# A gathered table as two float32r halves instead of three bfloat16 parts, in a graph network on one Trainium2 core

## The chip, the cores and the metric

The kernel runs on one core of one Trainium2 chip. The core has five engines that run their own instruction streams: TensorE (PE) multiplies, VectorE (DVE) and ScalarE (ACT) work elementwise, GpSimd (POOL) here issues the indirect transfers (gathers and scatters), and SyncE (SP) issues the plain ones. Sixteen DMA engines carry out all transfers. Tables between the stages lie in device memory (HBM); on the core there is the on-chip memory of 128 partitions and the accumulators (PSUM) that PE writes. The metric is the device time of one execution in microseconds; less is better.

## The reference, cut to what matters

Inputs are 6250 nodes of 256 features and a graph of 50,000 random pairs taken in both directions and 6250 self loops, 106,250 edges in all, sorted by their target node. There are four steps, each added to x:

```python
x = x + gnn0(layernorm(x), edges, ...)      # two sums over neighbours (256 and 512 wide), with dense layers
x = x + attention(layernorm(x), ...)        # slice tokens: 8 heads of 64 tokens over all nodes
x = x + gnn1(layernorm(x), edges, ...)      # one sum over neighbours, 256 wide
x = x + ffn1(layernorm(x), ...)             # the 2 best of 8 experts for each node

def gnn1(x, src, dst):
    src, dst = concatenate([src, loop]), concatenate([dst, loop])   # self loops once more
    h = x @ W
    deg = segment_sum(ones, dst); dinv = rsqrt(deg)
    out = segment_sum(h[src] * (dinv[src] * dinv[dst])[:, None], dst) + b
    return relu((out - running_mean) * rsqrt(running_var + eps) * gamma + beta)
```

The change concerns gnn1's sum over neighbours. The kernel first sums the rows of layernorm(x) times dinv[src] and multiplies by W afterwards, which gives the same.

## The kernel before, in words

Nodes are worked on in 49 tiles of 128, edges in chunks of 128. A sum over neighbours is made by PE: for one chunk, GpSimd gathers the 128 source rows into an on-chip tile (one edge per partition), VectorE makes a 128 x 128 matrix of zeros and ones that has a one where an edge goes to a node, and PE multiplies the two and accumulates over the chunks of a tile. So that bfloat16 products give a float32 result, a row of a table is stored as three bfloat16 parts that add up to the float32 number (`split`, L370), and each chunk takes three products (`multiply`, L179, its matmul in L183).

The class `Sums` (L187) does this for all three sums. It keeps a ring of on-chip tiles for gathered rows (`depth` of them, `message` L207). In `__call__` (L233) for a tile, gathers are issued ahead until chunk c + depth (L162 by way of L244); for every half-step k (some 8 chunks of targets from half a tile) `hot` (L219) makes the zeros and ones for its chunks with one VectorE instruction (L227); then come the products, and after the half-step `add` puts the sum where it belongs. Other work is let in between chunks through `between`.

The stages of the program are: layer norm and a plan of the edges (to 150 us); the first sum with its dense layers (to about 1330); the second sum, of which every third half-step gathers float32 rows and multiplies them as float32 (L253), with the logits and tokens of the attention (to about 2520); the core of the attention (to 2549); deslicing (to 2650); and the third stage (to the end).

Deslicing (the loop that ends in the write to T3, L1315 to L1335) goes over groups of four tiles: eight float32 products per pair of tiles (L1325), the addition to x1 (L1327), the layer norm times dinv, the `split` into three parts (two copies on ScalarE, L372 and L375, and two differences on VectorE, L373 and L376), and the write of the group to table T3 through ScalarE's queue (L1335). Each group's slice weights are loaded at its head.

The third stage runs in a block in which the order of SP, PE, ACT and DVE is the order written (`manual_schedule`); GpSimd's order is laid down by `in_order`. A ring of 14 tiles (`sums = Sums(others, T3, msgs, 14, ...)`, L1362) holds rows of T3. The self loops are not in the 782 chunks of this sum: each tile of sums `s3s[t]` is loaded ahead from S3, a table of zeros unless edges lie beyond the plan (`load_ahead`, 7 buffers), VectorE adds the tile's own rows to it (L1701), and `add3` (L1353 to L1359) the accumulated products. Two tiles at a time then pass through `choice`: transposes of s3 (L387), the product with W (`pn`, L1393), the layer norm, transposes, the product with the gate (`pg`, L1414), VectorE's choice of the two best experts, the places of the rows (`pp`, L1453), and four indirect writes of the rows into the experts' regions (`send`, L1472). As soon as an expert has 128 rows, a block is due: SP fetches its rows and biases (four blocks ahead), PE transposes (`pt`, L1579), multiplies by the first weights (`ph`, L1585), ScalarE copies and applies relu (L1587 to L1594), PE multiplies by the second (`py`, L1599), VectorE adds the bias (L1600) and SP stores the rows. There are 112 such blocks; their pieces are let in between the chunks, seven slots per tile. The eight experts' weights, 16 loads, come in at the stage's head. At the end GpSimd gathers for each tile the two rows of its experts' outputs (`g`, L1637, 8 buffers), and VectorE adds them with their shares (L1638).

Of the kernel before, what the change touches and what calls it, by code (L numbers as in the profile page):

```python
# [9 lines left out]
F32 = mybir.dt.float32  # L10
BF16 = mybir.dt.bfloat16
I32 = mybir.dt.int32
AF = mybir.ActivationFunctionType
OP = mybir.AluOpType
AX = mybir.AxisListType
# [2 lines left out]
P = 128  # L18
# [3 lines left out]
def gin_transolver_gcn_moe(ctx: ExitStack, tc: tile.TileContext, a: dict, out: bass.AP):  # L22
# [13 lines left out]
    nc = tc.nc  # L36
    x, src, dst = a["x"], a["src"], a["dst"]
    N, D = x.shape
# [32 lines left out]
    class Chunks:  # L71

        def __init__(self, edges):
            self.n, self.per = -(-edges // P), -(-edges // N)
            assert all(self.start(k) < self.start(k + 1) for k in range(2 * NT - 1))

        def start(self, k):

# [8 lines left out]
    T1 = dram.tile([NP, 3 * D], BF16, name="T1")  # L87
    T1f = dram.tile([NP, D], F32, name="T1f")
    T2 = dram.tile([NP, 3 * HID], BF16, name="T2")
    T3 = dram.tile([NP, 3 * D], BF16, name="T3")  # L90
    T2f = dram.tile([NP, HID], F32, name="T2f")
    kept = dram.tile([P, NCP], I32, name="kept_src"), dram.tile([P, NCP], F32, name="kept_dst")
    flat = [dram.tile([P, NCH2], F32, name="flat" + n) for n in ("src", "dst")]
# [93 lines left out]
    class Sums:  # L187
# [4 lines left out]
        def __init__(self, edges, table, pool, depth, hots, ps, add, ones=0, whole=None, is_whole=lambda k: k % 3 == 1):  # L192
            self.whole, self.whole_at = whole, is_whole
            self.edges, self.start = edges, edges.start
            self.table, self.hots, self.ps, self.add, self.ones = table, hots, ps, add, ones
            W = table.shape[1]
            self.F = W // 3
            self.ring = [pool.tile([P, W + 4 * ones], BF16, name=f"msg{i}") for i in range(depth)]
            self.of = [None] * depth
            self.hotf = None  # L200
            self.n, self.made, self.beside = 0, {}, None
            self.early, self.each = False, None
# [16 lines left out]
        def hot(self, k, c0):  # L219

            if (k, c0) not in self.made:
                n = min(HOTS, self.start(k + 1) - c0)
                if self.is_whole(k):
                    hot = self.hotf[k % 2] if self.hotf else self.hots.tile([P, HOTS, P], F32, name="hotf", bufs=2)
                else:
                    hot = self.hots.tile([P, HOTS, P], BF16, name="hot")
                nc.vector.scalar_tensor_tensor(  # L227
                    hot[:, :n, :], self.edges.dst[:, c0:c0 + n, None].to_broadcast([P, n, P]), float(k * HALF),
                    node2[:, k % 2, None, :].to_broadcast([P, n, P]), op0=OP.subtract, op1=OP.is_equal)
                self.made[k, c0] = hot  # L230
            return self.made[k, c0]

        def __call__(self, t, between=None, times=7):  # L233

            ks = range(2 * t, min(2 * t + 2, 2 * NT - 1))
            lo, hi = self.start(ks[0]), self.start(ks[-1] + 1)
            done = 0
            for k in ks:
                pa = self.ps.tile([P, 512], F32, name="pa", tag="agg", bufs=2)
                for c in range(self.start(k), self.start(k + 1)):  # L240
                    while self.n < min(c + len(self.ring), self.edges.n):
                        of = next(u for u in range(k, 2 * NT) if self.n < self.start(u + 1))
                        table = self.whole if self.is_whole(of) else self.table
                        ins = gather(self.message(self.n, of)[:, :table.shape[1]], table, self.edges.src[:, self.n:self.n + 1])  # L244
                        self.n += 1
                        if self.beside is not None:
                            in_order(ins)
                            self.beside(t)
                    c0 = c - (c - self.start(k)) % HOTS
                    hot, msg, ends = self.hot(k, c0)[:, c - c0, :], self.message(c, k), (c == self.start(k), c == self.start(k + 1) - 1)  # L250
                    if self.is_whole(k):
                        n = self.F + self.ones
                        self.last = nc.tensor.matmul(pa[:, :n], hot, msg[:, :n], start=ends[0], stop=ends[1])  # L253
                    else:
                        self.last = multiply(pa, hot, msg, self.F, *ends, self.ones)
                    if self.each is not None:
                        self.each(c)
                    if self.early and c == self.start(k) + 2 and k + 1 < 2 * NT - 1:
                        self.hot(k + 1, self.start(k + 1))
                    while between is not None and done < (c + 1 - lo) * times // (hi - lo):  # L260
                        between()
                        done += 1
                self.added = self.add(k, pa)
# [17 lines left out]
    def rest(table, add, n_of, count=None, begin=None, kept=None):  # L281


        n = nc.values_load(n_of[0:1, 0:1], min_val=0, max_val=NT)
        W = table.shape[1]
        with tc.tile_pool(name="rest", bufs=1) as w, tc.tile_pool(name="rest_ps", bufs=1, space=PSUM) as ps:
            with tc.For_i(0, n, 1) as t:
                t = nc.s_assert_within(t, 0, NT - 1)
                if begin is not None:
                    begin(t, w)  # L290
                src_of, dst_of = srcT, dstT
                if kept is not None:
                    src_of = w.tile([P, NCP], I32, name="srcT")
                    nc.sync.dma_start(src_of, kept[0])
                    dst_of = w.tile([P, NCP], F32, name="dstT")
                    nc.sync.dma_start(dst_of, kept[1])
                c0 = nc.values_load(bounds[0:1, ds(t, 1)], min_val=0, max_val=NCP)
                c1 = nc.values_load(bounds[0:1, ds(t + NT, 1)], min_val=0, max_val=NCP)
                with tc.For_i(c0, c1, 1) as c:
                    c = nc.s_assert_within(c, 0, NCP - 1)  # L300
                    ii = w.tile([P, 1], I32, name="ii")
                    nc.vector.tensor_copy(ii, src_of[:, ds(c, 1)])
                    parts_ = BF16 if table is not T1f else F32
                    msg = w.tile([P, W], parts_, name="msg")
                    gather(msg, table, ii)

                    k = w.tile([P, 8], F32, name="k")
                    nc.vector.tensor_tensor(k[:, 4:5], dst_of[:, ds(c, 1)], first[:, ds(t, 1)], op=OP.subtract)
                    hot = w.tile([P, P], parts_, name="hot")
                    nc.vector.tensor_scalar(hot, node, k[:, 4:5], None, op0=OP.is_equal)  # L310
                    pa = ps.tile([P, 512], F32, name="pa")
                    if parts_ is F32:
                        nc.tensor.matmul(pa[:, :W], hot, msg, start=True, stop=True)
                    else:
                        multiply(pa, hot, msg, W // 3, True, True)
                    add(t, pa, w)
                    if count is not None:
                        pc = ps.tile([P, 2], F32, name="pc")
                        nc.tensor.matmul(pc, hot, ones[:, :2], start=True, stop=True)
                        nc.vector.tensor_add(count[:, ds(t, 1)], count[:, ds(t, 1)], pc[:, 0:1])  # L320
# [26 lines left out]
    def layer_norm(work, xt, J, outs, times=None, sd=None, here=0):  # L347
# [14 lines left out]
        for j in range(J):  # L362
# [3 lines left out]
            else:  # L366
                nc.scalar.activation(outs[j], xt[:, j, :], AF.Identity, scale=sd[:, 0, j:j + 1],
                                     bias=sd[:, 1, j:j + 1])

    def split(parts, v, left, less):  # L370

# [659 lines left out]
    with tc.tile_pool(name="attn", bufs=1) as ap_:  # L1031
# [281 lines left out]
        with back, tc.tile_pool(name="desl_ps", bufs=2, space=PSUM) as ps:  # L1313
            w = bw
            for ts in groups(4, 5):  # L1315
# [4 lines left out]
                for j0 in range(0, J, 2):  # L1320
                    js = range(j0, min(j0 + 2, J))
                    p = ps.tile([P, 2, D], F32, name="po", tag="mm", bufs=4)
                    for j in js:
                        for m in range(KG):
# [4 lines left out]
                hs = w.tile([P, 4, D], F32, name="hs")  # L1329
                layer_norm(w, x1, J, [hs[:, j, :] for j in range(J)], dinv[:, ts[0]:ts[-1] + 1],  # L1330
                           ln3[:, :, ts[0]:ts[-1] + 1])
                hr = w.tile([P, 4, 3, D], BF16, name="hr")
                for _ in split(hr[:, :J], hs[:, :J, :], hs[:, :J, :], nc.vector.tensor_tensor):
                    pass
                nc.scalar.dma_start(block(T3, ts), hr[:, :J].rearrange("p j s f -> p j (s f)"))  # L1335
    right.close()
    effs.close()
# [21 lines left out]
            nc.vector.tensor_add(s3s[t][rows], s3s[t][rows], pa[rows, :D])  # L1359

    start = others.start
    sums = Sums(others, T3, msgs, 14, hots, ps, add3)  # L1362
    sent = [[] for _ in parts]
    taken = [[] for _ in parts]
    stored = [[] for _ in parts]
# [5 lines left out]
    def load_ahead(t):  # L1371

        for u in range(t, min(t + 5, NT)):
            if u not in s3s:
                s3s[u] = w.tile([P, D], F32, name="s3", bufs=7)
                nc.sync.dma_start(s3s[u], S3[u])

    def flush(keep):
# [246 lines left out]
    def combine(when):  # L1625
# [3 lines left out]
        o = xr[:r, t, :]  # L1629
        gs = []  # L1630
        for c in range(2):
            g = w.tile([P, D], F32, name="g", bufs=8)
            in_order(gather(g[:r], XD[i], place[:r, t, c:c + 1]))
            gs.append(g[:r])

# [119 lines left out]
```

## Time and profile before

| | us |
|---|---|
| median of three runs | 4216.75 (4215.5 to 4220.2) |
| profiled execution | 4227.88 |
| its span in the profile | 4225.7 |
| deslicing | 2549 to 2650 |
| third stage | 2650 to 4226 |

Mean granted clock of PE in the profiled execution: 0.838 of full speed.

How to read the lines: L183 is line 183 of the kernel. A group of instructions shows the engine, the operation, what it writes and reads by the program's names, the tile's shape and type, how often it occurs, then its busy time in us, the mean of one in ns, and the idle time of the engine ahead of it with what ended that time. PEld is PE's loading of weights (here the ones and zeros), which can lie beside a product. "Issue" is time in which the engine waited for nothing that the profile shows; "remote" is an event whose sender the profile doesn't show. In the page's rows of 40 slices each digit is the busy tenths of one slice (106 us), and PEclk the clock that was granted to PE, in tenths of full speed. A line of the waits gives the total us, the number of waits and the longest. A line of the timeline gives the start, the length, the engine and the number of instructions run together, and in brackets what ended the idle time before.

### The profile page before, as it was taken

How to read it: one execution, taken by the hardware profiler on the slowest of the kernel's cores; microseconds unless marked ns; L12 is line 12 of the kernel's file. 1: busy time of each engine (PE TensorE's matmuls, PEld its weight loads, DVE VectorE, ACT ScalarE, POOL GpSimd, SP SyncE). 2: the span in 40 equal slices, each digit the busy share in tenths (PEclk: the TensorE clock that was granted, in tenths of full speed). 3: DMA queues.
4: the chain of work that ended last, by engine and by line, in shares of the span. 5: the costliest groups of instructions: out<-in, count | busy, mean ns of one | idle time of the engine just before them, and what ended most of it. 6: DMA issues, size and time to landing. Idle time of an engine off the chain costs nothing. (4 is left out here: it accounts for less than half of the span.)

```text
span 4225.7 us, 42390 instructions
## 1 busy us (share of the span) xinstructions
PE 3043.9 (72%) x12790; PEld 1826.7 (43%) x12854; DVE 1553.9 (37%) x3988; ACT 863.7 (20%) x1737; POOL 2510.3 (59%) x2618
## 2 busy tenths in 40 slices
PE   3667777777786788788878779345677767667775
PEld 2334433333343444444444447234445545445543
DVE  5353222122222444344444447233333333333343
ACT  4111111111121111111111125011222222222332
POOL 4776666666664666666666630665656665666544
PEclk6788888888898889899988989667888888888977
DMA  7567767777676778777877755645545555555545
GB/s 257 164 209 230 223 219 231 221 222 220 219 241 245 262 265 262 247 252 260 272 254 248 245 170 178 223 136 149 157 147 152 153 158 153 155 158 163 158 123 154
DMA packets 356496, 861.49 MB, mean 204 GB/s; under 512 B 60104, under 2 KB 158674, under 8 KB 356266
## 3 DMA queue, kind: packets, MB, share of 16 engines
q0 software_dynamic: 174688, 611.60, 47.3%
q1 hardware_dynamic: 175066, 237.50, 16.4%
q10 hardware_dynamic: 6512, 9.63, 0.6%
q8 instruction: 106, 1.74, 0.2%
q14 instruction: 124, 1.02, 0.1%
HBM read 691.29 MB, written 167.21 MB: 203 GB/s over the span
## 5 line engine op out<-in xcount | busy, mean ns | idle before, releaser
L162 POOL DMA_INDIRECT msg<-T,srcT x2059 | 1976.5, 960 | 1363.3 <-issue 549.1
L183 PE MATMUL pa<-msg,hot 128*128 128x257 bf16 (+2 forms) x6114 | 1135.6, 323 | 194.0 <-issue 101.0
L183 PEld LDWEIGHTS <-hot 128*128 128x128 bf16 x6177 | 650.8, 106 | 795.1 <-issue 536.4
L162 POOL DMA_INDIRECT msg<-T2f,srcT x256 | 242.9, 949 | 138.8 <-PE pa L183 60.1
L1599 PE MATMUL py<-wx,hT 128*128 x896 | 257.0, 438 | 94.3 <-issue 90.5
L227 DVE SCALAR_TENSOR_TENSOR hot<-dstT,node 128x1024 bf16<-128x1024 f32 (+2 forms) x255 | 310.4, 1219 | 30.7 <-PE pa L183 20.1
L928 PE MATMUL p<-W2a,h2T 128*128 128x512 f32 x392 | 233.2, 679 | 66.6 <-issue 38.7
L1599 PEld LDWEIGHTS py<-wx,hT 128*128 128x128 f32 x896 | 197.9, 224 | 182.7 <-issue 149.6
L1585 PE MATMUL ph<-wx,xdT 128*128 x448 | 253.6, 695 | 28.9 <-ACT xdT L1581 13.3
L642 DVE TENSOR_TENSOR dinv<-dinv,pa 128x1 f32<-128x1 f32 x145 | 22.2, 153 | 658.9 <-PE pa L183 361.5
L253 PE MATMUL pa<-msg,hotf 128*128 128x512 f32 x512 | 255.9, 625 | 0.6 <-issue 0.3
L919 PE MATMUL p<-h1T,W1b 128*128 128x512 f32 (+2 forms) x480 | 221.1, 559 | 40.6 <-issue 21.4
L1600 DVE TENSOR_TENSOR yd<-py,wb 128x256 f32<-128x256 f32 x112 | 47.5, 425 | 435.7 <-PE py L1599 259.3
L1193 PE MATMUL ptok<-xn,sw 128*128 128x257 f32 (+1 forms) x392 | 123.8, 463 | 94.4 <-DVE sw L1182 47.2
L271 DVE SCALAR_TENSOR_TENSOR s<-s,own,pa 128x512 f32<-128x512 f32 x97 | 72.0, 742 | 224.2 <-PE pa L253 87.6
L1594 ACT ACTIVATE hT<-pt,wb 128x128 f32<-128x128 f32 x448 | 127.6, 369 | 126.0 <-remote 113.7
L909 PE MATMUL p<-h0T,W1a 128*128 128x512 f32 (+2 forms) x240 | 119.7, 598 | 43.9 <-issue 29.8
L1587 ACT ACTIVATE h<-ph 128x512 f32<-128x512 f32 x112 | 66.9, 598 | 405.7 <-remote 151.0
L1591 PE MATMUL pt<-ident,h 128*128 128x128 f32 x448 | 76.5, 297 | 101.0 <-ACT h L1587 57.7
L1193 PEld LDWEIGHTS ptok<-xn,sw 128*128 128x128 f32 (+1 forms) x392 | 87.7, 233 | 133.9 <-DVE sw L1182 55.8
L1168 PE MATMUL pl<-Weff,xnT 128*128 128x512 f32 x196 | 107.9, 691 | 47.3 <-issue 27.6
L162 POOL DMA_INDIRECT g<-XD,place x98 | 97.1, 991 | 70.5 <-DVE xr L1638 26.8
(379 smaller groups left out, 3644.4 us busy)
## 6 DMA issues: line engine op xcount, KB each, us to landing
XD<-zeros SPq DMA_DIRECT2D x204, 256.0 KB
msg<-T,srcT POOLq DMA_INDIRECT x2059
T<-tp SPq DMA_DIRECT2D x49, 384.0 KB
wb<-WB SPq DMA_DIRECT2D x112, 130.0 KB
xd<-XD SPq DMA_DIRECT2D x112, 128.0 KB
XD<-yd SPq DMA_DIRECT2D x112, 128.0 KB
T2f<-tf SPq DMA_DIRECT2D x49, 256.0 KB
s<-T2f SPq DMA_DIRECT2D x23, 512.0 KB
```

The source lines that it names most:

```text
L162: return nc.gpsimd.indirect_dma_start(out=msg, out_offset=None, in_=table, in_offset=bass.IndirectOffsetOnAxis(ap=ix, axis=0))
L183: ins = nc.tensor.matmul(pa[:, :n], hot, msg[:, s * F:s * F + n], start=(start and s == 2), stop=(stop and s == 1))
L227: nc.vector.scalar_tensor_tensor(hot[:, :n, :], self.edges.dst[:, c0:c0 + n, None].to_broadcast([P, n, P]), float(k * HALF), node2[:, k % ...
L253: self.last = nc.tensor.matmul(pa[:, :n], hot, msg[:, :n], start=ends[0], stop=ends[1])
L909: nc.tensor.matmul(p[:, :T], W1a[:, k, m * P:(m + 1) * P], h0T[:, k, :T], start=(k == 0), stop=(k == KD - 1))
L919: nc.tensor.matmul(p[:, :T], W1b[:, k, m * P:(m + 1) * P], h1T[:, k, :T], start=(k == 0), stop=(k == KH - 1))
L928: nc.tensor.matmul(p, h2T[:, k, j * P:(j + 1) * P], W2a[:, k, :], start=(k == 0), stop=(k == KH - 1))
L1168: nc.tensor.matmul(p, xnT[:, k, j * P:(j + 1) * P], Weff[:, k, :], start=(k == 0), stop=(k == KD - 1))
L1193: nc.tensor.matmul(p[:, :D + 1], sws[j][:r, m * P:(m + 1) * P], xn[:r, j, :], start=(j == 0), stop=(j == J - 1))
L1585: nc.tensor.matmul(p[:, :HID], xdT[:, k, :], W1[:, k, :], start=(k == 0), stop=(k == KD - 1))
L1594: nc.scalar.activation(hT[:, m, :], pt[:, m * P:(m + 1) * P], AF.Relu, bias=b1[:, m:m + 1])
L1599: nc.tensor.matmul(p[:, :D], hT[:, m, :], W2[:, m, :], start=(m == 0), stop=(m == KH - 1))
```

## The change

T3 holds float32 rows of 512 numbers, two halves of 256, instead of bfloat16 rows of 3 x 256: the first half is the number rounded to float32r, the second the difference from it, which float32r holds exactly. A row takes 2048 bytes instead of 1536. `halves_of` makes both with one copy and one difference per group of tiles. A chunk takes two products (`multiply_halves`) with ones and zeros in float32r. The ring has 10 tiles (of 2048 bytes) instead of 14 (of 1536). The tiles of ones and zeros hold `edges.most` chunks: 8 in the third sum, where they held 9 (`HOTS`), and 9 as before in the others. The tiles s3 and g share 8 buffers, where s3 had 7 and g 8. `rest` takes the new form too; it handles edges beyond the plan, of which these inputs have none.

```diff
+F32R = mybir.dt.float32r
...
+            self.most = -(-self.per // 2)
...
-    T3 = dram.tile([NP, 3 * D], BF16, name="T3")
+    T3 = dram.tile([NP, 2 * D], F32, name="T3")
...
-            self.F = W // 3
-            self.ring = [pool.tile([P, W + 4 * ones], BF16, name=f"msg{i}") for i in range(depth)]
+            self.halves = table.dtype == F32
+            self.F = W // 2 if self.halves else W // 3
+            self.ring = [pool.tile([P, W + 4 * ones], table.dtype, name=f"msg{i}") for i in range(depth)]
...
-                n = min(HOTS, self.start(k + 1) - c0)
+                n = min(self.edges.most, self.start(k + 1) - c0)
...
-                    hot = self.hots.tile([P, HOTS, P], BF16, name="hot")
+                    hot = self.hots.tile([P, self.edges.most, P], F32R if self.halves else BF16, name="hot")
...
+                    elif self.halves:
+                        self.last = multiply_halves(pa, hot, msg, self.F, *ends)
...
+    def multiply_halves(pa, hot, msg, F, start, stop):
+
+        for s in range(2):
+            ins = nc.tensor.matmul(pa[:, :F], hot, msg[:, s * F:(s + 1) * F].bitcast(F32R),
+                                   start=(start and s == 0), stop=(stop and s == 1))
+        return ins
+
+    def halves_of(parts, v):
+
+        nc.scalar.activation(parts[:, :, 0, :], v, AF.Copy)
+        nc.vector.tensor_tensor(parts[:, :, 1, :], v, parts[:, :, 0, :].bitcast(F32), op=OP.subtract)
...
-                hr = w.tile([P, 4, 3, D], BF16, name="hr")
-                for _ in split(hr[:, :J], hs[:, :J, :], hs[:, :J, :], nc.vector.tensor_tensor):
-                    pass
+                hr = w.tile([P, 4, 2, D], F32R, name="hr")
+                halves_of(hr[:, :J], hs[:, :J, :])
+                hr = hr.bitcast(F32)
                 nc.scalar.dma_start(block(T3, ts), hr[:, :J].rearrange("p j s f -> p j (s f)"))
...
-    sums = Sums(others, T3, msgs, 14, hots, ps, add3)
+    sums = Sums(others, T3, msgs, 10, hots, ps, add3)
...
-                s3s[u] = w.tile([P, D], F32, name="s3", bufs=7)
+                s3s[u] = w.tile([P, D], F32, name="s3", tag="s3", bufs=8)
...
-            g = w.tile([P, D], F32, name="g", bufs=8)
+            g = w.tile([P, D], F32, name="g", tag="s3", bufs=8)
```

More of the change, by code (lines that the diff above doesn't have):

```diff
@@ L221, in hot @@
             if (k, c0) not in self.made:
-                n = min(HOTS, self.start(k + 1) - c0)
+                n = min(self.edges.most, self.start(k + 1) - c0)
                 if self.is_whole(k):
-                    hot = self.hotf[k % 2] if self.hotf else self.hots.tile([P, HOTS, P], F32, name="hotf", bufs=2)
+                    hot = self.hotf[k % 2] if self.hotf else self.hots.tile([P, self.edges.most, P], F32, name="hotf", bufs=2)
                 else:
-                    hot = self.hots.tile([P, HOTS, P], BF16, name="hot")
+                    hot = self.hots.tile([P, self.edges.most, P], F32R if self.halves else BF16, name="hot")
                 nc.vector.scalar_tensor_tensor(
@@ L248, in __call__ @@
                             self.beside(t)
-                    c0 = c - (c - self.start(k)) % HOTS
+                    c0 = c - (c - self.start(k)) % self.edges.most
                     hot, msg, ends = self.hot(k, c0)[:, c - c0, :], self.message(c, k), (c == self.start(k), c == self.start(k + 1) - 1)
@@ L302, in rest @@
                     nc.vector.tensor_copy(ii, src_of[:, ds(c, 1)])
-                    parts_ = BF16 if table is not T1f else F32
+                    parts_ = table.dtype
                     msg = w.tile([P, W], parts_, name="msg")
@@ L308, in rest @@
                     nc.vector.tensor_tensor(k[:, 4:5], dst_of[:, ds(c, 1)], first[:, ds(t, 1)], op=OP.subtract)
-                    hot = w.tile([P, P], parts_, name="hot")
+                    hot = w.tile([P, P], F32R if table is T3 else parts_, name="hot")
                     nc.vector.tensor_scalar(hot, node, k[:, 4:5], None, op0=OP.is_equal)
                     pa = ps.tile([P, 512], F32, name="pa")
-                    if parts_ is F32:
+                    if table is T1f:
                         nc.tensor.matmul(pa[:, :W], hot, msg, start=True, stop=True)
+                    elif parts_ == F32:
+                        multiply_halves(pa, hot, msg, W // 2, True, True)
                     else:
```

## The prediction

> **What bounds the kernel now.** I read the page first, then the groups of instructions with their shapes kept apart in the third stage (2650 to 4226 us), then the waits of that stage, its chain, and last a timeline of some 30 us.
>
> The page's second part shows the stages as slices of 106 us:
>
> ```profile
> PE 3043.9 (72%) x12790; PEld 1826.7 (43%) x12854; DVE 1553.9 (37%) x3988; ACT 863.7 (20%) x1737; POOL 2510.3 (59%) x2618
> ...
> PE   3667777777786788788878779345677767667775
> ...
> POOL 4776666666664666666666630665656665666544
> PEclk6788888888898889899988989667888888888977
> DMA  7567767777676778777877755645545555555545
> ```
>
> No engine is full. In the third stage (slices 25 to 40) PE is at 6 to 7 tenths, POOL at 5 to 6, DMA at 4 to 5: something alternates. The windows (us, then busy PE, weight loads, DVE, ACT, POOL, then clock, DMA share, GB/s) say the same of deslicing and of the stage's three parts:
>
> ```profile
> 2549.00:2650.00 101.00, 84.82 (x392) 74.34 (x392) 73.73 (x200) 55.31 (x95) 0.00 (x0) 0.94 0.57 192
> 2650.00:2900.00 250.00, 113.96 (x573) 75.58 (x573) 76.91 (x255) 23.30 (x43) 160.27 (x169) 0.64 0.57 176
> 2900.00:3990.00 1090.00, 772.84 (x3873) 555.05 (x3873) 415.12 (x1534) 271.87 (x658) 660.60 (x693) 0.83 0.53 156
> ```
>
> The groups of the third stage that the change touches:
>
> ```profile
> L162 POOL DMA_INDIRECT msg<-T,srcT x782 | 742.6, 950 | 658.9 <-issue 292.0 <-PE pa L183 180.8 <-remote 140.0
> L183 PE MATMUL pa<-msg,hot 128*128 128x256 bf16 x2346 | 354.7, 303 | 89.9 <-issue 34.4 <-DMA msg<-T,srcT 25.0 <-DMA s<-S 20.3
> L183 PEld LDWEIGHTS <-hot 128*128 128x128 bf16 x2346 | 253.5, 109 | 174.7 <-issue 89.8 <-DVE hot L227 22.5 <-DVE s L1359 7.4
> ```
>
> 782 chunks over 24.5 pairs of tiles are 31.9 per pair, and a pair takes about 57 us (1090 us hold 19.1). GpSimd issues per pair 31.9 gathers and 4 sends, 0.95 us each and 0.3 us of issue behind it: 36 x 1.255 = 45.2 us. What it waits for in 2900 to 3990:
>
> ```profile
> POOL msg L162 <- PE pa L183: 154.7, 123, 6.1
> POOL msg L162 <- remote: 111.5, 71, 2.9
> POOL msg L162 <- issue: 102.4, 332, 0.7
> ```
>
> The first line, less the 0.3 us of issue in each of its waits, is some 6.8 us per pair in which the ring of 14 is full: GpSimd's slack is 12% of a pair, so it is nearly as tight as PE. The chain of 3288 to 3990 (702 us, 12.3 pairs) passes through both:
>
> ```profile
> by line: issue 18.0%; PE py L1599 17.1%; another core or an unknown queue 15.9%; PE ph L1585 14.1%; PE pa L183 13.8%; PE pt L1591 3.5%; PE pt L387 2.4%; PE pn L1393 2.1%; PE pt L1579 2.0%; PE pg L1414 1.5%; ACT xn L345 1.0%; DVE pn L1396 0.
> ```
>
> 13.8% of 702 us is 97 us, 7.9 us per pair, of the 14.0 us that L183's products last (268.2 us in 1090). So 0.56 of them are on the path. "Issue" and "unknown queue" are stalls of about 20 us per pair, in which PE, DVE, ACT and GpSimd all stand and resume together. The timeline shows one, and the run of products before it:
>
> ```profile
> 3322.39 4.51 PE L183 MATMUL pa<-msg,hot 128*128 128x256 bf16 x36
> 3328.53 0.94 POOL L162 DMA_INDIRECT msg<-T,srcT  x1 [0.30 <-issue]
> 3331.56 0.87 DVE L1359 TENSOR_TENSOR s<-s,pa 64x256 f32<-64x256 f32 x2 [6.67 <-remote]
> 3331.64 0.94 POOL L162 DMA_INDIRECT msg<-T,srcT  x1 [2.17 <-remote]
> ```
>
> Twelve chunks are multiplied without a break once per pair. Counting gathers against chunks done, the lead stands at 14 before this burst and at 5 when POOL has begun to refill; in the first five pairs (2690 to 2870 us), where the gathers share the DMA engines with the expert loads, it falls to between 0 and 4.
>
> **The change, part by part.** The sum is made against the profiled execution, 4227.88 us (span 4225.7 and 2.2 around it), which lies 11.1 us (0.26%) above the median 4216.75; differences are carried to the median unchanged.
>
> *Products.* Groups of 6, 9 and 36 bf16 products last 0.82, 1.15 and 4.51 us: 0.11 us each between the first two, 0.124 between the last two, so 0.33 to 0.37 us per chunk. No row shows a float32r product. Bounds: two at the bf16 spacing (0.22; one pass of the same 256 columns) and two at what float32 takes:
>
> ```profile
> L1325 PE MATMUL po<-M,swT 128*128 128x256 f32 x392 | 84.9, 379 | 0.9 <-ACT M L1308 0.9
> L1325 PEld LDWEIGHTS po<-M,swT 128*128 128x128 f32 x392 | 74.4, 190 | 11.5 <-ACT M L1308 1.4
> ```
>
> 84.9 / 392 = 0.217 us for a float32 record, 0.43 for two. I take 0.22, as one record per product is what the program holds now, and keep 0.43 as a rival. A third of the 7.9 us on the path would go. The burst, 4.5 of them, is set by the ring (below); the rest gives (7.9 - 4.5) / 3 = 1.1 us, x 24.5 = -28 us. Bounds: -65 (all 7.9) and the rival's loss.
>
> *Weight loads.* A bf16 load lasts 109 ns and a float32 load 190, and in the float32 group above the 190 ns loads lie inside records that follow each other every 217 ns, so I cost them at nothing; bare, they would make a chunk 2 x (0.19 + 0.11) = 0.60 us, 0.27 above now. The Trainium skill, "TensorE: Matmul & The Clock Gate", section "Weight-path perf modes — Fast Weight Load (FWL) and DoubleRow", says that fast loading of weights is on for 128 weights of a type other than FP32; it speaks against this change: if a float32r load counts as FP32 and is not covered, the sum would hold 0.27 x 31.9 x 0.56 x 24.5 = +118 us by it, where the row has 0.
>
> *The ring, 14 to 10.* A gather lands 2.7 to 3.0 us after it starts, and gathers start 1.255 apart. Of the burst's 12 chunks 10 are there; chunks 11 and 12 can be gathered when slots 1 and 2 are free, at 0.3 and 1.55 us, and land near 3.2 and 4.5 us (a little later with longer rows): the burst ends at 5.2 to 5.5 us instead of 4.5. +1.0 us in 19.5 pairs, +19.5. In the five early pairs the lead of 0 to 4 falls short by some 2 chunks of 4: 2 x 1.255 = 2.5 us each, +12.5. Together +32. Bounds: 0 (a lead of 5 less 4 is still 1, and the burst isn't waited for) and 4 x 1.255 x 24.5 = +123. Because it holds fewer ahead, GpSimd issues the four sends of a pair four gathers (5 us) earlier against the gathers; the block fetches behind them wait for fresh rows only at the end, so this is 0, or -5 at best.
>
> *Longer rows.* GpSimd's own time per gather does not follow the row: 2048-byte rows of the second table took 949 ns against 950 here.
>
> ```profile
> L162 POOL DMA_INDIRECT msg<-T2f,srcT x256 | 242.9, 949 | 138.8 <-PE pa L183 60.1 <-issue 50.9 <-remote 11.4
> ```
>
> Each of the 16 DMA engines' packets of one gather last 477 ns in all now (2 x 178 and 1 x 121); as four pieces of the 159 ns that 4096-byte packets take they last 636. DMA's share rises from 0.53 to about 0.62: not full, but each wait for a landing is longer. Some four per pair (the burst's end, three lockstep resumptions) by 0.2 us: +20. Bounds 0 and 4 x 1.0 (a third of 3.0) x 24.5 = +98. At the stage's head the engines are full (share 1.06 at 2660 to 2680, where the experts' weights load), and 40 gathers bring 1.3 MB more at 371 GB/s: 3.5 us, and the table's last block a little; +5 (0 to +20, the wait for S there).
>
> *One-hot tiles, split, buffers.* Float32 one-hots cost DVE what bf16 did, so 0:
>
> ```profile
> L227 DVE SCALAR_TENSOR_TENSOR hot<-dstT,node 128x1024 bf16<-128x1024 f32 x201 | 242.6, 1208 | 20.1 <-PE pa L183 20.1
> L227 DVE SCALAR_TENSOR_TENSOR hotf<-dstT,node 128x1024 f32<-128x1024 f32 x32 | 38.4, 1201 | 0.0
> ```
>
> The split loses 15 copies and 15 differences; deslicing runs at PE's pace (84.9 us back to back), which hides all but those behind the last product (2635 to 2647 us, of which the four serial steps are 0.45 to 1.2 us each): -3.5 us (0 to -5). The writes of the third table grow by a third, beside the products: 0, or +2 in the tail. s3 and g share 8 buffers for 15: the first g is gathered at 4039.6 us, after the last addition to s3 (4011.9), so 0; if s3 were refilled later than now, it would be +1 per pair.
>
> Sum: -3.5 - 28 + 32 + 20 + 5 = +25.5, so **4242 us** on the median (4253 for the profiled execution).
>
> **The rivals.** *A, the forecast:* the ring and the longer rows eat the saving, 4225 to 4262 us; chance 0.36.
>
> *B, the saving passes (faster):* PE sets the pair, POOL's 6.8 us of full ring become the reserve, and products that are a third shorter shorten the path by up to 2.6 us per pair: -65 - 3.5 = -68; with the ring and landings taking a third of it, -40, 4177 us. For it: L183 on the chain at 13.8%, GpSimd waiting for pa 154.7 us. Against it: the same wait says that GpSimd has only 12% to give. It decides if chunks 11 and 12 land within the burst or after work of the blocks. 0.34.
>
> *C, float32r at float32's pace:* 0.43 us a chunk, +0.1 x 31.9 x 0.56 x 24.5 = +44, with ring +15, landings and head +25, split -3.5: about +80, 4297 us. For it: the only measured products of 4-byte operands run so. Against: one record per product. 0.12.
>
> *D, stalls of their own:* the lockstep stalls come about every nine GpSimd transfers; if a ring of 10 makes one more of 2.2 to 2.9 us per pair, that is +54 to +71 on top of A's sum, 4296 to 4313 us. Nothing in the trace names their cause. 0.08.
>
> *E, all of it beside other work:* within 8 us of before. 0.10.
>
> **How the numbers follow.** A is likeliest, so 4242. Slower: A, C and D, less 0.02 of A that lies near the bound, 0.54; faster: B and 0.02 of E, 0.36; same: the rest of E and that of A, 0.10, which is within 0.2% (8.4 us), about what a measurement of this kernel can tell from no change. Leaving out the best tenth of B (under 4165) and the worst tenth (most of C's upper half, over 4305) gives 4165 to 4305; A's own range is 4225 to 4262.
>
> **What the trace after would show.** Products: 0.22 us a chunk in the burst if right, 0.43 in C, 0.60 if loads show. Ring: GpSimd's waits for pa grow above 154.7 us, and PE has waits for the landing of msg in steady pairs, where it has none now; in B they don't appear and the pair falls to 54 us. Rows: landing 0.16 to 0.3 us later, DMA share 0.6. Deslicing should end 3 to 4 us earlier. The forecast is wrong if the lockstep stalls change in number or length, since 20 us of each pair hang on them, or if the early pairs lose far more than 2.5 us each.

## The result and the profile after

The change made the kernel slower: 4268.31 us (median of 10 runs, 4251.94 to 4286.79) against 4217.44 us, a ratio of 1.0113 with a 95% interval of 1.0097 to 1.0128, some 48 us. The profiled execution took 4255.06 us, 13 under its median, with a span of 4253.3 us.

The chips differ. The later runs name theirs: on chips 1 and 11 the kernel before takes 4227 us, much as on the chip of the result (4217), and on chips 3 and 0 it takes 3572 to 3575 us. I call these the first and the second kind of chip. What makes the difference is not known. Every ratio below is against the kernel before on the same chip. Five of the later kernels were measured on the second kind only, and the change once more there.

The page of the changed kernel, its busy times and two of its rows of 40 slices:

```profile
PE 2986.7 (70%) x12008; PEld 1835.4 (43%) x12072; DVE 1534.2 (36%) x3973; ACT 855.1 (20%) x1722; POOL 2500.9 (59%) x2618
...
PE   3667777777686888888888887456666566656775
...
POOL 4776666666664666666666611665555655555544
```

PE is 57 us less busy and the program is longer. In slices 30 to 37 PE stands at 5 to 6 where it stood at 6 to 7, and POOL is a tenth lower in three of them: more of the stage is idle on both. The window of the steady part says how much (columns: us, busy PE, weight loads, DVE, ACT, POOL, clock, DMA share, GB/s):

```profile
2900.00:3990.00 1090.00, 683.42 (x3067) 521.43 (x3067) 385.15 (x1422) 257.74 (x614) 629.38 (x662) 0.78 0.62 185
```

PE's busy time falls from 773 to 683 us, and yet GpSimd gets 662 transfers done where it did 693. At 36 transfers per pair of tiles that is 59.3 us per pair instead of 56.6. Per pair PE is busy 37.2 us instead of 40.1, so the saving came, and idle 22.1 us instead of 16.5. From the first gather of the stage to the last, 1402.8 us passed instead of 1359.2, +43.6. None of it comes early: the product of chunk 256 stands 446 us behind the first gather, before it was 449; between chunk 256 and 736 it falls 39 us behind.

The changed groups in the third stage:

```profile
L164 POOL DMA_INDIRECT msg<-T,srcT x777 | 735.6, 947 | 543.7 <-PE pa L380 206.0 <-issue 167.7 <-remote 114.2
L380 PE MATMUL pa<-msg,hot 128*128 128x256 f32 x1562 | 348.4, 360 | 114.1 <-DMA msg<-T,srcT 89.3 <-issue 19.7 <-DVE hot L230 3.9
L380 PEld LDWEIGHTS pa<-msg,hot 128*128 128x128 f32 x1562 | 267.6, 233 | 161.2 <-DMA msg<-T,srcT 114.7 <-issue 34.0 <-DVE hot L230 4.2
```

A gather still takes GpSimd 0.95 us. That the busy time of the products' group hardly falls (354.7 to 348.4 us) does not mean that they are as slow: in this trace a float32r record that follows another kind of product starts mostly 0.02 to 0.07 us behind that product's start, a bfloat16 one 0.1 to 0.2 us behind it, so the group's time takes in work of the product ahead. The chain of 3300 to 4010 us and three of its longest pieces:

```profile
by line: another core or an unknown queue 25.7%; issue 15.0%; PE ph L1604 14.0%; PE py L1618 13.8%; PE pa L380 11.6%; DMA msg<-T,srcT 5.1%; PE pt L1610 3.7%; PE pt L406 2.6%; PE pn L1412 2.3%; PE pt L1598 1.7%; ACT h L1606 1.4%; PE pg L1433
...
3299.66 12.25 another core or an unknown queue x2
3477.09 12.28 another core or an unknown queue x2
3714.99 12.22 another core or an unknown queue x2
```

The products' share falls, from 13.8 to 11.6%. The unknown wait grows from 15.9 to 25.7%; the longest pieces last 12.2 us, and their starts lie multiples of some 59 us, a pair of tiles, apart. What stands in such a piece is seen in the timeline of three engines around 3300. PE and ACT:

```profile
3300.34 0.83 PE L380 MATMUL pa<-msg,hot 128*128 128x256 f32 x4
3301.01 0.60 PE L1610 MATMUL pt<-ident,h 128*128 128x128 f32 x4
3301.36 0.72 PE L380 MATMUL pa<-msg,hot 128*128 128x256 f32 x4
3312.32 3.78 PE L1618 MATMUL py<-wx,hT 128*128 x8 [10.24 <-ACT hT L1613]
...
3299.06 0.60 ACT L1606 ACTIVATE h<-ph 128x512 f32<-128x512 f32 x1 [1.30 <-PE ph L1604]
3311.90 1.14 ACT L1613 ACTIVATE hT<-pt,wb 128x128 f32<-128x128 f32 x4 [12.24 <-remote]
```

PE ends the transposes that ACT needs (L1610) at 3301.6, but ACT begins the step behind them at 3311.9, and PE then waits for ACT. GpSimd in the same time:

```profile
3296.08 0.94 POOL L164 DMA_INDIRECT msg<-T,srcT  x1 [1.46 <-PE pp L1472]
3297.33 0.95 POOL L164 DMA_INDIRECT msg<-T,srcT  x1 [0.30 <-issue]
3298.58 1.00 POOL L1491 DMA_INDIRECT XD<-xn,place  x1 [0.30 <-issue]
...
3308.78 0.95 POOL L164 DMA_INDIRECT msg<-T,srcT  x1 [0.30 <-issue]
3312.13 0.94 POOL L164 DMA_INDIRECT msg<-T,srcT  x1 [2.40 <-remote]
```

It issues eleven transfers in one run, from 3296.1 to 3309.7, the four sends in its middle, then pauses for 2.4 us; ACT goes on when this pause ends. The waits of the whole steady part say that this is the rule: ScalarE's second step waited 103.8 us in 19 waits, of at most 6.8 us, before, and after

```profile
ACT hT L1613 <- remote: 195.6, 18, 12.3
```

Behind the stall stands the run of products, and there the ring shows as the prediction had it: ten chunks without a break, then chunks 11 and 12, which wait for their landings.

```profile
3315.54 3.83 PE L380 MATMUL pa<-msg,hot 128*128 128x256 f32 x20
3320.28 0.50 PE L380 MATMUL pa<-msg,hot 128*128 128x256 f32 x2 [0.92 <-DMA msg<-T,srcT]
3322.20 0.50 PE L380 MATMUL pa<-msg,hot 128*128 128x256 f32 x2 [1.41 <-DMA msg<-T,srcT]
```

PE's waits for landings come to 44.2 us in 35 waits in the steady part, where there were none, and GpSimd's waits for `pa` grow from 154.7 to 179.1 us.

### The profile page after: what moved, and what is told of

It reads as the page before. It is cut to its first block, busy times and chain, and to the rows that moved or that the text cites. A ratio compares the mean times of both kernels' runs of the same rounds, so it can differ in the third digit from the quotient of the medians.

```text
span 4253.3 us, 40850 instructions
## 1 busy us (share of the span) xinstructions
PE 2986.7 (70%) x12008; PEld 1835.4 (43%) x12072; DVE 1534.2 (36%) x3973; ACT 855.1 (20%) x1722; POOL 2500.9 (59%) x2618
## 5 line engine op out<-in xcount | busy, mean ns | idle before, releaser
L185 PE MATMUL pa<-msg,hot 128*128 128x256 bf16 (+2 forms) x3768 | 777.7, 335 | 104.3 <-issue 69.7
L185 PEld LDWEIGHTS <-hot 128*128 128x128 bf16 x3831 | 397.1, 104 | 612.7 <-issue 436.7
L380 PE MATMUL pa<-msg,hot 128*128 128x256 f32 x1564 | 349.2, 360 | 132.7 <-DMA msg<-T,srcT 89.3
L380 PEld LDWEIGHTS pa<-msg,hot 128*128 128x128 f32 x1564 | 268.1, 233 | 180.2 <-DMA msg<-T,srcT 114.7
L230 DVE SCALAR_TENSOR_TENSOR hot<-dstT,node 128x1024 fp32r<-128x1024 f32 (+3 forms) x255 | 310.6, 1220 | 25.4 <-issue 16.9
L1604 PE MATMUL ph<-wx,xdT 128*128 x448 | 263.4, 719 | 52.1 <-ACT xdT L1600 26.2
L1610 PE MATMUL pt<-ident,h 128*128 128x128 f32 x448 | 77.5, 301 | 126.1 <-ACT h L1606 96.6
L1604 PEld LDWEIGHTS ph<-wx,xdT 128*128 128x128 f32 x448 | 94.0, 229 | 134.6 <-issue 103.6
L1415 DVE SCALAR_TENSOR_TENSOR pn<-pn,dinv,scale 128x256 f32<-128x256 f32 x49 | 24.0, 489 | 318.9 <-remote 263.3
```

The source lines that it names most:

```text
L185: ins = nc.tensor.matmul(pa[:, :n], hot, msg[:, s * F:s * F + n], start=(start and s == 2), stop=(stop and s == 1))
L230: nc.vector.scalar_tensor_tensor(hot[:, :n, :], self.edges.dst[:, c0:c0 + n, None].to_broadcast([P, n, P]), float(k * HALF), node2[:, k % ...
L380: ins = nc.tensor.matmul(pa[:, :F], hot, msg[:, s * F:(s + 1) * F].bitcast(F32R), start=(start and s == 0), stop=(stop and s == 1))
L1604: nc.tensor.matmul(p[:, :HID], xdT[:, k, :], W1[:, k, :], start=(k == 0), stop=(k == KD - 1))
L1610: nc.tensor.transpose(pt[:, m * P:(m + 1) * P], h[:, m * P:(m + 1) * P], ident)
```

## The experiments

Four theories stood for the 48 us: the ring's lost lead, the longer rows, the float32r form of the products, and products that are too short. The first four kernels take the change apart.

**The ring alone**

```diff
-    sums = Sums(others, T3, msgs, 14, hots, ps, add3)
+    sums = Sums(others, T3, msgs, 10, hots, ps, add3)
```

> The kernel before with a ring of 10 instead of 14, nothing else changed (three bfloat16 products, rows of 1536 bytes). By the prediction's sum the ring costs +32 us: +1.0 us per steady pair of tiles and +2.5 us in each of five early pairs. Rival, since the profile after shows the early pairs no later and the steady pairs 2.6 us longer: the ring alone costs 2 to 2.6 us in each steady pair, +38 to +50 us, all that the change lost. Second rival: the rows and not the ring do it, and this kernel stays within 8 us of before.

Measured on the first kind: 1.0014 (0.9998 to 1.0030), +6 us. Neither +32 nor +38; the second rival, within 8 us, holds. The lead falls to 2 chunks in each pair where it fell to 5. PE now waits 19.0 us in 31 waits for landings, about the forecast's 1.0 us per pair, but most of that does not reach the end.

**The rows alone**

```diff
-    T3 = dram.tile([NP, 3 * D], BF16, name="T3")
+    T3 = dram.tile([NP, 4 * D], BF16, name="T3")
...
-                hr = w.tile([P, 4, 3, D], BF16, name="hr")
+                hr = w.tile([P, 4, 4, D], BF16, name="hr")
+                nc.gpsimd.memset(hr[:, :J, 3, :], 0.0)
```

> The kernel before with rows of the third table of 2048 bytes (the three bfloat16 parts and a quarter that is zero and is not multiplied), ring of 14; to make room s3 and g share 8 buffers as in the change. It shows what longer rows cost alone. By the prediction's sum +25 us (landings +20, the stage's head +5). Rival: GpSimd's time per gather does not follow the row, and a lead of 5 chunks covers a landing that is 0.2 to 0.3 us later, so within 8 us of before.

Measured on the first kind: 1.0028 (1.0009 to 1.0046), +12 us. Half of the forecast's term.

**Ring and rows, products as before** (both edits above)

> Rows of 2048 bytes as in the kernel with long rows, and a ring of 10: all of the change but the float32r products and the shorter split. By the prediction's sum +57 us (32 for the ring, 25 for the rows), and the change itself would lie 32 us under this kernel. Rival: the products give nothing at the end, and this kernel is as slow as the change, +48 us; then the two have the same length of a pair of tiles.

Measured on the first kind: 1.0036 (1.0021 to 1.0051), +15 us, where the forecast's sum was +57 and the whole change +48. So ring and rows make a third of the loss, and by difference the products, which were to give 32 us back, make the rest. In its waits the landing of msg does appear at PE, as 17.8 us in 30 waits, and costs little; the step of ScalarE waits as before:

```profile
ACT hT L1595 <- remote: 99.8, 18, 6.7
```

**The products alone**

```diff
-    sums = Sums(others, T3, msgs, 10, hots, ps, add3)
+    sums = Sums(others, T3, msgs, 14, hots, ps, add3)
...
-    T3 = dram.tile([NP, 2 * D], F32, name="T3")
+    T3 = dram.tile([NP, 3 * D // 2], F32, name="T3")
...
-            ins = nc.tensor.matmul(pa[:, :F], hot, msg[:, s * F:(s + 1) * F].bitcast(F32R),
+            ins = nc.tensor.matmul(pa[:, :F], hot, msg[:, s * F // 2:s * F // 2 + F].bitcast(F32R),
```

> The changed kernel with rows cut to 1536 bytes and a ring of 14: the second product reads columns 128 to 384 of the row, so the second halves are multiplied from the wrong columns and the third sum is not right; number and size of the products are those of the change. It shows what two float32r products instead of three bfloat16 ones, with the shorter split, bring when ring and rows stay. By the prediction's terms -32 us without the burst's share, up to -68 us if all 7.9 us per pair on the path shrink by a third. Rival: the end is set by GpSimd and the stalls in lockstep, and the products' time only turns into more waiting: within 8 us of before.

Measured on the first kind: 1.0096 (1.0075 to 1.0117), +41 us. Both expectations fell, which had a gain and nothing. With the ring and the rows of before, two products per chunk are slower than three. Its profile has the same long wait as the change's, with a longer total:

```profile
ACT hT L1613 <- remote: 210.1, 19, 12.3
```

That left the form (4-byte operands, weight loads) against the number of products. Two kernels were to part them and two to try the ring further:

**Two bfloat16 products, three float32r products, a ring of 8 before and after the change**

```diff
-        for s in (2, 0, 1):
+        for s in parts:          # (0, 1) for T3, (2, 0, 1) for the other tables
```

```diff
-        for s in range(2):
+        for i, s in enumerate((0, 1, 1)):
```

```diff
-    sums = Sums(others, T3, msgs, 14, hots, ps, add3)
+    sums = Sums(others, T3, msgs, 8, hots, ps, add3)
```

> The kernel before with two bfloat16 products per chunk instead of three (the third, smallest part of the row is gathered and not multiplied); ring, rows, one-hots and split as before. Theory that shorter products are themselves the loss (they no longer fill the time in which PE's signals to the other engines stand still, and GpSimd's runs of transfers grow longer): slower than before by about what the float32r kernel with ring 14 and short rows lost, +30 to +50 us. Rival, that the float32r form is the loss (4-byte weight loads, one instruction for load and product): this kernel is not slower, between 0 and -40 us.

> The float32r kernel with ring 14 and rows of 1536 bytes, with a third float32r product per chunk (the second once more, so that the third sum is not right): as many products as before, 0.35 us a chunk. Theory of the short products: most of the +41 us goes, within 15 us of before. Rival of the float32r form: no faster than with two products, +41 us or more.

> The kernel before with a ring of 8. Ring of 10 cost 6 us. If a shorter ring only takes lead away, 8 costs more than 10: +15 to +40 us. If a shorter ring also shortens GpSimd's runs of transfers, and with them the stalls of the other engines, it is within 10 us of before or faster.

> The changed kernel with a ring of 8 instead of 10, products and rows as in the change. Lead alone: slower than the change, +60 to +90 us over before. If the long runs of GpSimd's transfers make the stalls: runs of 11 to 14 become shorter, and it is faster than the change, +10 to +40 us over before.

Measured on the second kind: 1.0004 (0.9995 to 1.0014), 1.0001 (0.9991 to 1.0011), 1.0096 (1.0079 to 1.0112, +34 us) and 1.0166 (1.0149 to 1.0183, +59 us). The loss that they were to explain doesn't occur there, so they don't tell the two theories apart; they show what the stage is without its stalls. GpSimd's waits between 2400 and 3300 us, of the kernel with two bfloat16 products:

```profile
POOL msg L162 <- issue: 73.8, 242, 0.3
POOL msg L162 <- PE pa L183: 39.0, 128, 0.3
```

No wait is longer than the 0.3 us that follow every transfer: it issues without a pause, its 36 transfers of 1.255 us per pair are the bound, and neither the number nor the form of the products reaches the end. There the lead counts: a ring of 8 costs 34 us, with pauses in GpSimd's work again.

**Two bfloat16 products and the change again**

> Two bfloat16 products instead of three, once more. On the chip of the last call, where the kernel before takes 3575 us, GpSimd issued its 713 transfers of the middle of the third stage without one pause and the number of products made no difference. Where the kernel before takes some 4220 us, as it did for the prediction: short products as the loss give +30 to +50 us, the float32r form as the loss gives 0 to -40 us. Where it takes some 3575 us: 0 again.

> The changed kernel, unaltered, beside the one with two bfloat16 products. Where the kernel before takes some 4220 us: +48 us again. Where it takes some 3575 us and GpSimd sets the pace, products hidden: the ring of 8 cost 32 us there with short rows and 62 us with long ones, so a ring of 10 with long rows costs +5 to +30 us, by the lead alone.

Measured, on the second kind: 1.0003 (0.9993 to 1.0013) and 1.0081 (1.0063 to 1.0099), +29 us, at the upper end of what was expected. The second one is the changed kernel itself, so its trace can be laid beside that of the first kind. GpSimd is busy as long (2507 and 2501 us), but the span is 3607.5 and not 4253.3 us, and ScalarE's step waits only for the transposes that it needs, 2.0 us at most (2600 to 3300 us):

```profile
ACT hT L1613 <- PE pt L1610: 30.4, 15, 2.0
```

**Ring, rows and two bfloat16 products together**, the edits of the kernels above:

> All of the change but the float32r form and the shorter split: rows of 2048 bytes, a ring of 10, s3 and g sharing 8 buffers, and two bfloat16 products per chunk (the third, smallest part isn't multiplied). Where the kernel before takes some 4220 us: if short products are the loss, as slow as the change, +35 to +55 us; if the float32r form is the loss, no slower than the same kernel with three products (+15 us), -20 to +20 us. Where the kernel before takes some 3575 us: as the change there, +29 us, if ring and rows make it; less than +15 us if the float32r form has a part in it.

Measured, on the second kind: 1.0070 (1.0057 to 1.0084), +25 us. So there the change's loss is ring and rows, and float32r has no part in it that can be seen (the intervals overlap).

**A table of two bfloat16 parts, ring 14**

```diff
-    T3 = dram.tile([NP, 3 * D], BF16, name="T3")
+    T3 = dram.tile([NP, 2 * D], BF16, name="T3")
...
-                hr = w.tile([P, 4, 3, D], BF16, name="hr")
-                for _ in split(hr[:, :J], hs[:, :J, :], hs[:, :J, :], nc.vector.tensor_tensor):
-                    pass
+                hr = w.tile([P, 4, 2, D], BF16, name="hr")
+                nc.scalar.activation(hr[:, :J, 0, :], hs[:, :J, :], AF.Copy)
+                nc.vector.tensor_tensor(hr[:, :J, 1, :], hs[:, :J, :], hr[:, :J, 0, :], op=OP.subtract)
```

> The kernel before with a third table of two bfloat16 parts (rows of 1024 bytes, one copy and one difference per group, two products per chunk), ring of 14: the numbers keep the first 16 bits of their mantissa, the third part is left out. Where the kernel before takes some 4220 us: short products as the loss, +25 to +45 us; the float32r form as the loss, 0 to -30 us, as the longer rows cost 12 us there. Where it takes some 3575 us: GpSimd sets the pace of the pairs of tiles, so only the stage's head, where transfers share the engines with the experts' weights, can gain: 0 to -15 us.

Measured on the first kind: 1.0073 (1.0051 to 1.0095), +31 us, with no float32r in it, shorter rows and the ring of before. This kernel has less work than the one before in products, rows and split, and it is slower. So the float32r form is not needed for the loss. This kernel and the one with the products alone share the two products per chunk and the shorter split, which lies in deslicing, outside the pairs that became longer; so the small number of products is what costs on the first kind. No kernel that changes that number and nothing else was measured there, and how much of the loss is PE's clock, 0.76 to 0.78 in the steady part with two products and 0.81 to 0.83 with three, was not parted from the waits. The wait is there again:

```profile
ACT hT L1594 <- remote: 215.8, 19, 12.5
```

**What the long waits have in common.** In the steady part (2900 to 3990 us) of the kernels on the first kind of chip I counted GpSimd's runs of transfers without a pause (starts at most 1.6 us apart) and PE's idle gaps:

| kernel | products per chunk | runs of 10 or more | PE gaps of 8 us or more | PE's gaps over 0.5 us, sum | us over before |
|---|---|---|---|---|---|
| before | 3 | 2 | 1 | 312 | 0 |
| ring 10 | 3 | 1 | 0 | 304 | 6 |
| long rows, ring 14 | 3 | 2 | 1 | 320 | 12 |
| long rows, ring 10 | 3 | 1 | 0 | 299 | 15 |
| float32r, short rows, ring 14 | 2 | 33 | 20 | 416 | 41 |
| the change | 2 | 33 | 16 | 402 | 48 |
| two bfloat16 parts, ring 14 | 2 | 32 | 20 | 408 | 31 |

With three products the typical long run has 8 or 9 transfers, with two it has 11 to 14, about twice per pair of tiles, and about once per pair PE stands for 8 us or more. The event records of the float32r kernel with ring 14 show what happens within one long wait: PE's transposes ended at 3323.2 us; the updates of PE's semaphore after that appear at 3323.5, 3324.9, 3326.3 and 3327.8, about one to each transfer that GpSimd issues, and the next three together at 3333.47 to 3333.56, in GpSimd's pause; ScalarE, which waited for them, starts at 3333.5. These records have gaps: with the changed kernel the first kind's trace has 880 updates of ScalarE's semaphore for 1546 instructions that raise it, the second kind's 1547. So the wait itself is sure, and that one update passed with each transfer is only what the records show. From the end of PE's transposes to ScalarE's step 0.98 us pass at the median in the changed kernel and 10.4 us at most; on the second kind, in the same kernel between 2600 and 3300 us, 0.09 and 2.6 us. There GpSimd has no pause in hundreds of transfers with a ring of 14, often runs 32 or more without one with shorter rings, and PE has no gap of 8 us. What holds the signals up on the first kind, and why not on the second, is open.

## Why the prediction was right, and where not

The direction and the range held, in part by luck. The measured 4268 us lies 26 us above the forecast's 4242 and above rival A's own range (4225 to 4262); the whole range reaches so far because of rivals C and D, neither of which came as described. The sum did not hold by its parts. It had +57 for ring and rows and -31.5 for products and split; measured one by one they are +15 and +41. Two errors of opposite sign, 42 and 72 us, partly made up for each other.

- *Products*, -28 us. This is the step that failed: "A third of the 7.9 us on the path would go." The work went (PE is busy some 3 us less per pair) and the idle time grew by more (5.6 us), in the long stalls of the table above. The shares of the chain don't show this alone: with the shorter ring alone, which lost 6 us, L183 also falls to 11.1% and the unknown wait rises to 21.1%. I had written that stalls of 20 us per pair lie on the path and that the forecast is wrong if their number or length changes, but priced the products as if the stalls stood still.
- *The pace of a product.* Taken as 0.22 us per chunk. Groups of 4 and 6 records behind the same kind of product last 0.72 and 0.95 us, so 0.23 for a chunk at full clock. Rival C, float32's 0.43, is out. PE's granted clock in the steady part was 0.78, before 0.83.
- *Weight loads*, 0. A load takes 233 ns on average against 109 for bfloat16. But the loads lie beside the products, as the 0.23 us per chunk shows, and the +118 us of bare loads did not come. The Trainium skill, "TensorE: Matmul & The Clock Gate", section "Weight-path perf modes — Fast Weight Load (FWL) and DoubleRow", gives fast loading to 128 weights of a type other than FP32; the 233 ns agree with that if float32r counts as FP32.
- *The ring*, +32. It measured +6 (-1 to +13). The early pairs, set at +12.5, lost nothing. The burst's wait came, +1.0 us per pair, but was added to the end as if PE had nothing else to wait for. On the second kind, without stalls, a ring of 8 costs 34 us, so there the lead counts. The 6.8 us per pair of full ring was also too much: the line gives (154.7 - 123 x 0.3) / 19.1 = 6.2.
- *Rows*, +25. Measured +12 (+4 to +19). The DMA share is 0.62 as forecast. One term of the sum was too small: 40 gathers of rows that are 512 bytes longer bring 2.6 MB more and not 1.3, which at 371 GB/s is 7 us and not 3.5.
- *One-hots*, 0, held: VectorE's mean over all forms is 1220 ns, before 1219. *Deslicing*, -3.5: from the start of its last product to the first gather 14.9 us instead of 16.6, so -1.7.
- *Rival B*, the saving passes, is wrong on both kinds of chip: on the first the stalls took it, on the second GpSimd is the bound and two products for three changed nothing (1.0004). *Rival D* came nearest to the cause, that the stalls grow, but had one more stall per pair where they became longer, and laid it to the ring: with that alone there is one run of ten or more, as against 33 in the change.

That more transfers fall into one run because PE, with shorter products, has freed more ring slots and reached the sends before GpSimd's next pause, is argued from the timeline, not shown. Kernels that break the runs at a fixed length were not tried, and no kernel here beat the one before.

## What to carry to other kernels

When several engines stand still together and the profile names no cause, the time that an engine saves must be priced with these stalls in view: first find, in one of them, who finished, who waits and which engine was busy throughout. An edit that only takes work away can lose, as two products for three did here; test it by taking the same work away in another form, which here cleared the number type in one run. And look which chip a ratio is from before two ratios are put side by side.

## What the runs showed of the hardware

On the first kind of chip ScalarE went on about 1 us after PE had ended the transposes that it waited for, and up to 10.4 us after while GpSimd issued indirect transfers in runs of 11 to 14 without a pause; on the second kind it was 0.09 us at the median in the same kernel. The kernel before took 3572 to 3575 us there against 4217 to 4227. The trace of the first kind also records fewer updates of the semaphores than there are instructions that raise them (880 for 1546 on ScalarE), the trace of the second kind as many (1547). A float32r product of 256 columns takes one record, with starts 0.115 to 0.125 us apart at full clock where bfloat16 has 0.109, about half of a float32 record's 0.217.
